# Offset convolution by minimal filtering of row pairs in a deformable-convolution kernel

## Chip, cores and metric

The kernel runs on one core of one Trainium2 chip. The metric is the device time of one execution in microseconds (us); the kernel before takes 1758.54 us (median of 3 runs, 1754.74 to 1759.95). The profiled execution spans 1756.5 us, and all times on the page count from its start. Engines: PE is TensorE (PEld its weight loads), DVE VectorE, ACT ScalarE, POOL GpSimd, SP the engine that issues most DMAs.

## What is computed

Two layers on a batch of 8 images of 128 channels and 64 x 64 pixels, all float32. Only the first is touched. Its steps, cut to what matters:

```python
xn  = group_norm(x)                                  # per image
om  = conv3x3(xn, off_w) + off_b                     # 128 -> 27 channels: THE OFFSET CONVOLUTION
off = om[:, :18].reshape(B, 9, 2, H, W)              # dy, dx of each of 9 taps at each pixel
mask = sigmoid(om[:, 18:])
py, px = row + ky - 1 + off_y, col + kx - 1 + off_x  # where each tap samples
val = bilinear(xn, py, px) * mask                    # 4 corners, zero outside the image
y   = einsum('bckhw,ock->bohw', val, w) + b          # deformable convolution, 128 -> 128
x   = x + relu(batch_norm(y) * gamma + beta)
# second layer: group norm, a 3x3 convolution with routed and mixed expert weights, residual
```

## The kernel before

The first layer is `dense()`. Each image is cut into 11 bands of 6 rows and each band into 11 blocks of 6 columns. For one block DVE multiplies row and column tents into sampling weights (`weights`), PE multiplies them with the block's pixels (`sample`), ACT copies the samples out of PSUM, and PE makes the deformable convolution of the band before (`conv`). The tents come from the offsets, through tables in device memory. The offset convolution and these tables are made by a generator, `tables(b)`, of which a step or two is taken in each block, so that the tables of an image are made while the image before it is sampled; image 0's run alone at the start.

```python
def weights(n):                                    # DVE, one per block
    s = a6.tile([P, TAPS, T, T], F32, name="s")    # a6: 6 buffers
    nc.vector.tensor_tensor(s[0:QQ], x_wts[...], y_wts[...], ALU.mult)

def sample(n):                                     # PE and ACT, one per block
    nc.tensor.matmul(pq, lhsT=xts[g][0:QQ, c], rhs=s, start=True, stop=True)
    nc.scalar.copy(samples[g % 2][...], pq)

def finish(g, py):                                 # one per band
    y = a3.tile([P, T, W], F32, name="y")          # a3: 3 buffers
    nc.scalar.activation(y[:, first:], py[:, first:], AF.Identity, bias=db_sb)
    yield
    nc.vector.bn_stats(ystats[:, b, j, :], flat)
    ...                                            # and the DMA of y to device memory

for g in range(len(bands) + 1):                    # the band loop
    ...
    for c in range(NT1):                           # 11 blocks
        weights(n + AHEAD)                         # AHEAD = 3
        sample(n)
        ...                                        # loads of the tables two bands ahead (POOL)
        next(ended, None)                          # a step of finish(g - 1)
        if g and c > 1:
            conv(g - 1, c - 2, py)
        next(turned, None)                         # pixels of band g + 1: transposes on PE
        for _ in range(1 + (c % 3 == 2)):          # 14 steps of tables in a band
            next(made, None)
```

The part of `tables(b)` that the change replaces, with what stands around it. `pad` holds the image, normalised in place, with rows of zeros above and below. Four matmuls with 32 output partitions each fill the four quarters of one PSUM tile, one for each quarter of the image:

```python
# ... load of the image, its statistics, scale and shift
for c in range(0, NCH, 2):                         # NCH = 8, 512 pixels each
    nc.scalar.activation(part[c], part[c], AF.Identity, bias=shift, scale=scale)
    nc.vector.tensor_scalar(part[c + 1], part[c + 1], scale, shift, ALU.mult, ALU.add)
    yield
if b == 0:
    for t in (y_wts[1], x_wts[1], x_wts[2]):
        nc.vector.memset(t, 0.0)
yield from pause(2)
def evacuate(c, pc):
    nc.scalar.activation(omr[:, c * CH : (c + 1) * CH], pc, AF.Identity, bias=offb_sb)
    nc.vector.tensor_scalar(omc[:, :, 8 * c : 8 * c + 8], pc.rearrange(...), offb_sb, None, ALU.add)
done = []
for c in range(2):
    pc = ps_c.tile([P, CH], F32, name="pc")
    for n, k in enumerate((4, 3, 5, 1, 0, 2, 7, 6, 8)):
        ...
        if n == 2 and done:
            evacuate(*done.pop())
        for j in range(4):
            r = 16 * j + 8 * c + ky + ROWPAD - 1
            nc.tensor.matmul(pc[32 * j : 32 * j + 32]..., lhsT=offw_sb[:, k, :],
                             rhs=pad[:, r : r + 8, lo + kx - 1 : hi + kx - 1],
                             start=(n == 0), stop=(n == TAPS - 1))
        if n % 2:
            yield from pause(5)
    yield from pause(3)
    done.append((c, pc))
evacuate(*done.pop())
yield from pause(4)
# ... DMAs of omr and omc to device memory, the reduction `most`, pause(9),
# ... loads into off_y, mask, off_x, pause(14), sigmoid of the mask,
for i in range(NR):                                # 5 tents: two ops of ACT, three of DVE,
    ...                                            # two stores each, two double buffers, 4 steps
```

Of the kernel before, what the change touches and what calls it, by code (L numbers as in the profile page):

```python
# [8 lines left out]
F32 = mybir.dt.float32  # L9
I32 = mybir.dt.int32  # L10
AF = mybir.ActivationFunctionType
ALU = mybir.AluOpType
# [4 lines left out]
P = 128  # L17
H = W = 64
HW = H * W
HP = WP = H + 2  # L20
TAPS = 9
NT = HW // P
CH = 512
# [22 lines left out]
WB = W + 2  # L46
ROWPAD = REACH + 1
NQI = H + 2 * ROWPAD
YSTEP = TAPS * WB
# [4 lines left out]
WP6 = W + 2 * ROWPAD  # L54
# [3 lines left out]
def deform_moe_conv(  # L58
# [18 lines left out]
    nc = tc.nc  # L77
# [91 lines left out]
    def dense():  # L169

        with ExitStack() as st:
            st.enter_context(tc.manual_schedule())
            a1 = st.enter_context(tc.tile_pool(name="d1", bufs=1))
            a2 = st.enter_context(tc.tile_pool(name="d2", bufs=2))
            a3 = st.enter_context(tc.tile_pool(name="d3", bufs=3))
            a6 = st.enter_context(tc.tile_pool(name="d6", bufs=6))
            ps_c = st.enter_context(tc.tile_pool(name="ps_c", bufs=2, space=PSUM))
            ps_q = st.enter_context(tc.tile_pool(name="ps_q", bufs=3, space=PSUM))
            ps_y = st.enter_context(tc.tile_pool(name="ps_y", bufs=1, space=PSUM))
# [9 lines left out]
                nc.gpsimd.memset(t[:, NT1 - 1, :, Q - ROWPAD :], 0.0)  # L189
            offw_sb = a1.tile([P, TAPS, 32], F32, name="offw_sb")  # L190
            nc.gpsimd.memset(offw_sb[:, :, 27:32], 0.0)
            offb_sb = a1.tile([P, 1], F32, name="offb_sb")
            nc.gpsimd.memset(offb_sb, 0.0)
            ident = a1.tile([P, P], F32, name="ident")
# [6 lines left out]

            off_y = a1.tile([WB, 3, 3, WB], F32, name="off_y")
            mask = a1.tile([WB, 3, 3, WB], F32, name="mask")
            off_x = a1.tile([WB, TAPS * (WP6 - 1) + ROWPAD], F32, name="off_x")
            for t in (off_y, mask, off_x):
                nc.gpsimd.memset(t, 0.0)


            x_wts = [a1.tile([P, NT1, T, TAPS, T], F32, name=f"xwts{i}") for i in range(3)]
            y_wts = [a1.tile([P, T, TAPS, WB], F32, name=f"ywts{i}") for i in range(2)]
# [10 lines left out]
            def tables(b):  # L223
# [4 lines left out]
                def pause(n):  # L228
                    for _ in range(n):
                        yield  # L230
# [3 lines left out]
                pad = pads[b % 2]  # L234
                others = (nc.sync, nc.sync) if b else (nc.scalar, nc.gpsimd)
                for q in range(4):
                    rows = slice(16 * q, 16 * q + 16)
# [39 lines left out]
                for c in range(0, NCH, 2):  # L277
# [2 lines left out]
                        part[c + 1], part[c + 1], scale, shift, ALU.mult, ALU.add  # L280
                    )
                    yield
                if b == 0:
                    for t in (y_wts[1], x_wts[1], x_wts[2]):
                        nc.vector.memset(t, 0.0)
                yield from pause(2)

                om = a1.tile([P, 2, HW // 4], F32, name="om", tag="om")
                omr = om[:, 0]
                omc = om[:, 1].rearrange("p (w h) -> p w h", w=W)  # L290

                def evacuate(c, pc):
                    nc.scalar.activation(
                        omr[:, c * CH : (c + 1) * CH], pc, AF.Identity, bias=offb_sb
                    )
                    nc.vector.tensor_scalar(
                        omc[:, :, 8 * c : 8 * c + 8],
                        pc.rearrange("p (h w) -> p w h", w=W),
                        offb_sb, None, ALU.add,
                    )  # L300

                done = []
                for c in range(2):
                    pc = ps_c.tile([P, CH], F32, name="pc")

                    for n, k in enumerate((4, 3, 5, 1, 0, 2, 7, 6, 8)):
                        ky, kx = divmod(k, 3)
                        lo, hi = max(0, 1 - kx), min(W, W + 1 - kx)
                        if n == 2 and done:
                            evacuate(*done.pop())  # L310
                        for j in range(4):
                            r = 16 * j + 8 * c + ky + ROWPAD - 1
                            nc.tensor.matmul(  # L313
                                pc[32 * j : 32 * j + 32].rearrange("p (h w) -> p h w", w=W)[
                                    :, :, lo:hi
                                ],
                                lhsT=offw_sb[:, k, :],
                                rhs=pad[:, r : r + 8, lo + kx - 1 : hi + kx - 1],
                                start=(n == 0),
                                stop=(n == TAPS - 1),  # L320
                                skip_group_check=True,
                            )
                        if n % 2:
                            yield from pause(5)
                    yield from pause(3)
                    done.append((c, pc))
                evacuate(*done.pop())
                yield from pause(4)
                for j in range(4):
                    nc.sync.dma_start(  # L330
# [7 lines left out]
                nc.vector.tensor_reduce(  # L338
                    most[:, b : b + 1], omr, AX.X, ALU.max, apply_absolute_value=True
                )  # L340
                yield from pause(9)
                for k in range(3):
                    rows = slice(k, k + H)
# [23 lines left out]
                else:  # L367
                    tents = []
                    for t in samples:
                        flat = t.rearrange("p k r w -> p (k r w)")  # L370
# [169 lines left out]

            LOADS = 17
            made, later = tables(0), tables(1)
            for _ in range(LOADS):
                next(made)
# [5 lines left out]
            def reach():  # L550
# [6 lines left out]
                nc.vector.tensor_reduce(count, pn[0:1], AX.X, ALU.add)  # L557
                nc.vector.tensor_copy(count_i, count)

            nc.sync.dma_start(out=dw_sb, in_=dw)  # L560
            for t, src in ((db_sb, db), (gamma_sb, gamma), (beta_sb, beta)):
                nc.sync.dma_start(out=t, in_=src)
# [20 lines left out]
            for g in range(len(bands) + 1):  # L583
                b, j = bands[g] if g < len(bands) else (B, 0)
                if g:
                    py = ps_y.tile([P, T, W], F32, name="py")
                if j == NT1 - 2:
                    for _ in made:
                        pass
                    made = tables(b + 2) if b + 2 < B else iter(())  # L590
                turned = pixels(g + 1) if g + 1 < len(bands) else iter(())
                for c in range(NT1):
                    if g < len(bands):
                        n = g * NT1 + c
# [260 lines left out]
    def layer1():  # L855
# [6 lines left out]
        with ExitStack() as st:  # L862
# [266 lines left out]
            for f, *args in todo:  # L1129
                f(*args)  # L1130

    dense()
    layer1()
    near_all = nc.values_load(count_i[0:1, 0:1], min_val=0, max_val=18 * 4 * B)
# [53 lines left out]
```

## Time and profile before

All times are of the profiled execution.

| stretch (us from the start) | what runs | PE busy | DVE busy |
|---|---|---|---|
| 0 to 76 | image 0: load, normalisation, offset convolution, tables | 23.16 | 29.75 |
| 76 to 1370 | the 88 bands, with the tables of images 1 to 7 in the first 76 of them | 1277.35 | 855.23 |
| 1370 to 1427 | start of the second layer | 20.57 | 48.37 |
| 1427 to 1757 | second layer | 322.50 | 256.34 |

How to read it. The page gives busy time for each engine, then the span in 40 slices, where a digit is the busy share in tenths; then the chain of work that ended last, as shares of the span. A row of the groups names line, engine, operation, output and inputs with partitions x elements, and the count; behind the bar are busy time and the mean of one in ns; behind the second bar the time for which the engine was idle just before, and what ended it. A float32 matmul stands in the trace as two instructions, so its counts are doubled. In a timeline each row is a start, a duration, the engine and the instruction, with equal neighbours merged.

### The profile page before, as it was taken

What the parts mean: (1) busy time and instruction counts of PE and PEld (TensorE: products, weight loads), DVE (VectorE), ACT (ScalarE), POOL (GpSimd) and SP (SyncE); (2) the same over time, 40 slices, a digit from 0 to 9 for tenths busy, and PEclk for the clock granted to TensorE, in tenths of its full rate; (3) what the DMA queues carried; (4) which work ended last, traced back from release to release, by engine and by line L of the source; (5) the groups of instructions that cost most, each with busy time, mean ns of one, the idle gap of its engine ahead of it and who ended that gap; (6) DMA issues with size and microseconds to landing.
All of it is one profiled execution on the core that took longest, in us unless ns stands there. A gap on an engine that the chain in (4) does not pass through costs nothing. (4 is left out here: it accounts for less than half of the span.)

```text
span 1756.5 us, 21264 instructions
## 1 busy us (share of the span) xinstructions
PE 1643.6 (94%) x6490; PEld 931.0 (53%) x6490; DVE 1189.7 (68%) x1910; ACT 944.4 (54%) x1970; POOL 939.6 (53%) x1516
## 2 busy tenths in 40 slices
PE   4399999999999999999999999999999479999998
PEld 2155565566566556655665666566666234444443
DVE  4464874687467648755874587477665688888882
ACT  1465765576476557655765676476665323333330
POOL 3375576558557746764675657557763322322210
PEclk9599999999999999999999999999999689999999
DMA  4643774585368438744863675376663603444311
GB/s 133 124 121 93 154 179 106 115 194 137 93 133 203 121 82 168 180 106 103 193 150 94 134 187 143 98 137 151 161 158 87 267 25 144 155 156 154 123 49 62
DMA packets 197598, 235.84 MB, mean 134 GB/s; under 512 B 133964, under 2 KB 148048, under 8 KB 197478
## 3 DMA queue, kind: packets, MB, share of 16 engines
q0 software_dynamic: 94976, 124.94, 32.4%
q1 hardware_dynamic: 100556, 109.04, 20.7%
q8 instruction: 57, 0.93, 0.2%
q10 hardware_dynamic: 1946, 0.41, 0.1%
q14 instruction: 63, 0.52, 0.1%
HBM read 183.00 MB, written 50.82 MB: 133 GB/s over the span
## 5 line engine op out<-in xcount | busy, mean ns | idle before, releaser
L495 DVE TENSOR_TENSOR s<-xwts,ywts 100x324 f32<-100x324 f32 x968 | 691.5, 759 | 186.4 <-PE pq L506 160.1
L506 PE MATMUL pq<-s,xt 100*128 100x324 f32 x1936 | 696.8, 441 | 12.4 <-DVE s L495 6.7
L512 ACT COPY samples<-pq 128x324 f32<-128x324 f32 x968 | 423.9, 443 | 463.8 <-PE pq L506 458.1
L521 PE MATMUL py<-samples,dw_sb 128*128 128x384 f32 (+1 forms) x1584 | 625.1, 476 | 2.2 <-ACT y L532 2.1
L441 POOL DMA_DIRECT2D xwts<-tabx x863 | 527.2, 621 | 96.9 <-DMA ywts<-taby 52.6
L425 POOL DMA_DIRECT2D ywts<-taby x528 | 302.4, 587 | 365.8 <-DVE s L495 309.4
L506 PEld LDWEIGHTS pq<-s,xt 100*128 100x128 f32 x1936 | 322.4, 190 | 185.9 <-issue 48.7
L521 PEld LDWEIGHTS py<-samples,dw_sb 128*128 128x128 f32 x1584 | 299.5, 189 | 138.5 <-ACT y L532 6.5
L478 PE MATMUL pt<-ident,picked 128*100 128x128 f32 x968 | 194.2, 275 | 41.8 <-ACT picked L465 33.7
L478 PEld LDWEIGHTS pt<-ident,picked 128*100 128x100 f32 x968 | 121.6, 128 | 181.7 <-issue 80.0
L535 DVE BATCH_NORM_STATS2 ystats<-y 128x6 f32<-128x384 f32 (+1 forms) x88 | 48.2, 547 | 218.5 <-ACT y L532 218.5
L1102 PE MATMUL pc<-v,u 128*128 128x512 f32 x384 | 172.8, 599 | 9.2 <-DVE u L1051 9.2
L1102 PE MATMUL pc<-v,wmix 128*128 128x512 f32 x384 | 176.4, 605 | 0.0
L485 ACT COPY xt<-pt 100x512 f32<-100x512 f32 (+1 forms) x264 | 147.5, 559 | 2.2 <-PE pt L478 2.2
L313 PE MATMUL pc<-pad,offw_sb 128*32 128x504 f32 (+1 forms) x1152 | 142.2, 601 | 1.9 <-ACT pad L278 1.9
L1102 PEld LDWEIGHTS pc<-v,u 128*128 128x128 f32 x384 | 72.4, 190 | 98.3 <-issue 85.1
L1080 ACT ACTIVATE t<-pc,bmix 128x512 f32<-128x512 f32 x32 | 22.0, 687 | 182.5 <-issue 94.3
L1102 PEld LDWEIGHTS pc<-v,wmix 128*128 128x128 f32 x384 | 72.3, 191 | 88.6 <-issue 84.9
L457 ACT COPY picked<-pad 128x900 f32<-128x900 f32 x88 | 91.7, 1042 | 9.0 <-DMA xwts<-tabx 9.0
L608 ACT COPY samples<-samples 128x1188 f32<-128x1188 f32 x80 | 95.9, 1198 | 0.0
L930 POOL TENSOR_TENSOR x<-x,xt 128x512 f32<-128x512 f32 x32 | 47.0, 1496 | 85.3 <-ACT x L928 85.3
L930 POOL TENSOR_TENSOR pad<-pad,pad 128x512 f32<-128x512 f32 x28 | 39.6, 1442 | 71.6 <-ACT pad L928 71.5
(137 smaller groups left out, 897.1 us busy)
## 6 DMA issues: line engine op xcount, KB each, us to landing
ywts<-taby POOLq DMA_DIRECT2D x528, 116.0 KB, 4.3
pad<-in_x_dram SPq DMA_DIRECT2D x48, 512.0 KB
xwts<-tabx POOLq DMA_DIRECT2D x173, 116.0 KB, 3.8
out_dram<-yo SPq DMA_DIRECT2D x32, 512.0 KB
xwts<-tabx POOLq DMA_DIRECT2D x172, 92.8 KB, 3.8
yd<-y SPq DMA_DIRECT2D x80, 192.0 KB
xwts<-tabx POOLq DMA_DIRECT2D x173, 69.6 KB, 3.6
pad<-yd SPq DMA_DIRECT2D x16, 512.0 KB
```

Source lines behind the costliest of these rows:

```text
L313: nc.tensor.matmul(pc[32 * j : 32 * j + 32].rearrange("p (h w) -> p h w", w=W)[:, :, lo:hi], lhsT=offw_sb[:, k, :], rhs=pad[:, r : r + 8, ...
L425: engine.dma_start(out=y_wts[g % 2][r * Q : (r + NR) * Q, r].rearrange("p b c -> p (b c)"), in_=bass.AP(tensor=y_table[b].tensor, offset=y ...
L441: engine.dma_start(out=x_wts[g % 3][q:QQ:Q, :, lo:hi].rearrange("p t a b c -> p t (a b c)"), in_=bass.AP(tensor=x_table[b].tensor, offset= ...
L457: nc.scalar.copy(picked[g % 2][:, 1 : NT1 - 1], bass.AP(tensor=one.tensor, offset=one.offset, ap=[list(one.ap[0]), [T, NT1 - 2], [W, Q], [ ...
L478: nc.tensor.transpose(pt[0:QQ, c], picked[g % 2][:, c0 + c].rearrange("p y x -> p (y x)"), ident,)
L485: nc.scalar.copy(xts[g][0:QQ, c0 : c0 + n], pt[0:QQ, 0:n])
L495: nc.vector.tensor_tensor(s[0:QQ], x_wts[g % 3][0:QQ, c].rearrange("p a k r -> p k r a"), y_wts[g % 2][0:QQ, :, :, T * c : T * c + T].rear ...
L506: nc.tensor.matmul(pq.rearrange("p k r a -> p (k r a)"), lhsT=xts[g][0:QQ, c], rhs=ss.pop(n)[0:QQ].rearrange("p k r a -> p (k r a)"), star ...
L512: nc.scalar.copy(samples[g % 2][:, :, 2 : T + 2, T * c : T * c + T], pq)
L521: nc.tensor.matmul(py[:, first:], lhsT=dw_sb[:, 3 * ky + kx], rhs=samples[g % 2][:, n, first + ky : T + ky, kx : kx + W], start=(i == 0), ...
L608: nc.scalar.copy(samples[g % 2][:, :, 0:2], samples[(g - 1) % 2][:, :, T : T + 2])
L1102: nc.tensor.matmul(pc, lhsT=us[j][:, kx], rhs=vs[g][:, rows, kx : kx + W], start=(kx == 0), stop=(kx == 2),)
```

## The change

For two output rows that lie below each other, a filter of three rows needs four input rows d0 to d3. Written out, that is six products with filter rows g0, g1, g2. Minimal filtering does it with four:

```
m0 = (d0 - d2) * g0            m1 = (d1 + d2) * (g0 + g1 + g2) / 2
m2 = (d2 - d1) * (g0 - g1 + g2) / 2            m3 = (d1 - d3) * g2
even row = m0 + m1 + m2        odd row = m1 - m2 - m3
```

Each product is a convolution along the row with three taps. In place of 2 chunks x 9 taps = 18 groups of four matmuls for an image there are 4 products x 3 taps = 12, of the same shape. It is for relieving PE. The row combinations (d0 - d2 and so on) are made by DVE, in two halves of 1024 elements for each product, and the four products are put together by ACT (one) and DVE (four operations); the copy `omc`, transposed within the tile, is made by ACT in one piece. The combined weights are made once, by POOL.

Two combination buffers of 8 KB in each partition need room: `off_y`, `mask` and `off_x` become views of one of them, and the buffers of `s` go from 6 to 5, those of `y` from 3 to 2. The zeroing of the three vanishes; the zeroing of other weight tiles moves behind the offset convolution of image 0. The second layer is untouched.

```diff
-            a3 = st.enter_context(tc.tile_pool(name="d3", bufs=3))
-            a6 = st.enter_context(tc.tile_pool(name="d6", bufs=6))
+            a3 = st.enter_context(tc.tile_pool(name="d3", bufs=2))
+            a6 = st.enter_context(tc.tile_pool(name="d6", bufs=5))
@@
+            offu_sb = [a1.tile([P, 3, 32], F32, name=f"offu_sb{i}") for i in range(2)]
@@
-            off_y = a1.tile([WB, 3, 3, WB], F32, name="off_y")
-            mask = a1.tile([WB, 3, 3, WB], F32, name="mask")
-            off_x = a1.tile([WB, TAPS * (WP6 - 1) + ROWPAD], F32, name="off_x")
-            for t in (off_y, mask, off_x):
-                nc.gpsimd.memset(t, 0.0)
+            combos = [a1.tile([P, H // 2, W], F32, name=f"combo{i}") for i in range(2)]
+            flat = combos[1].rearrange("p h w -> p (h w)")
+            off_y, mask = (flat[0:WB, i * YSTEP : (i + 1) * YSTEP]... for i in range(2))
+            off_x = flat[0:WB, 2 * YSTEP : ...]
@@ in tables(b): evacuate() and the loop over chunks and taps go; instead
+                two = omr.rearrange("p (t i w) -> p t i w", i=2, w=W)
+                even, odd = two[:, :, 0], two[:, :, 1]
+                def combine(j):                      # DVE, two halves, one step each
+                    lo, hi, op = ((0, 2, ALU.subtract), (1, 2, ALU.add),
+                                  (2, 1, ALU.subtract), (1, 3, ALU.subtract))[j]
+                    for half in range(2):
+                        rows = [pad[:, ROWPAD - 1 + H // 2 * half + i :][:, 0 : H // 2 : 2]
+                                for i in (lo, hi)]
+                        nc.vector.tensor_tensor(combo_of[j][:, half * n : half * n + n], *rows, op)
+                        yield
+                combo_of = {1: combos[0], 2: combos[1], 0: combos[0], 3: combos[1]}
+                weight_of = {0: offw_sb[:, 0:3], 1: offu_sb[0], 2: offu_sb[1], 3: offw_sb[:, 6:9]}
+                def tap(j, kx):                      # PE, four matmuls
+                    ...
+                        nc.tensor.matmul(pcs[j][32 * q : 32 * q + 32]..., lhsT=weight_of[j][:, kx],
+                            rhs=combo_of[j][:, 8 * q : 8 * q + 8, lo + kx - 1 : hi + kx - 1],
+                            start=(kx == 1), stop=(kx == 2))
+                for j in (1, 2):
+                    yield from combine(j)
+                yield from pause(2)
+                tap(1, 1); tap(1, 0)                 # (written on one line here)
+                yield from pause(6)
+                tap(1, 2); tap(2, 1)
+                yield from pause(3)
+                nc.scalar.activation(even, taken(1), AF.Identity, bias=offb_sb)
+                yield from combine(0)
+                yield
+                tap(2, 0); tap(2, 2)
+                yield from pause(3)
+                m2 = taken(2)
+                nc.vector.tensor_tensor(odd, even, m2, ALU.subtract)
+                nc.vector.tensor_tensor(even, even, m2, ALU.add)
+                yield
+                yield from combine(3)
+                tap(0, 1); tap(0, 0)
+                yield from pause(6)
+                tap(0, 2); tap(3, 1)
+                yield from pause(3)
+                nc.vector.tensor_tensor(even, even, taken(0), ALU.add)
+                yield from pause(3)
+                tap(3, 0); tap(3, 2)
+                yield from pause(4)
+                nc.vector.tensor_tensor(odd, odd, taken(3), ALU.subtract)
+                yield
+                nc.scalar.copy(omc, omr.rearrange("p (h w) -> p w h", w=W))
                 yield from pause(4)
@@ the zeroing of y_wts[1], x_wts[1], x_wts[2] (image 0) moves behind the reduction `most`
@@ once, at the start
+            u1, u2 = offu_sb
+            nc.gpsimd.tensor_tensor(u2, offw_sb[:, 0:3], offw_sb[:, 6:9], ALU.add)
+            nc.gpsimd.tensor_tensor(u1, u2, offw_sb[:, 3:6], ALU.add)
+            nc.gpsimd.tensor_tensor(u2, u2, offw_sb[:, 3:6], ALU.subtract)
+            for u in offu_sb:
+                nc.gpsimd.tensor_scalar(u, u, 0.5, None, ALU.mult)
```

## Prediction, made before the changed kernel ran

> **What bounds the kernel now.** I read the page from the slices down. Rows of section 2:
>
> ```profile
> PE   4399999999999999999999999999999479999998
> DVE  4464874687467648755874587477665688888882
> PEclk9599999999999999999999999999999689999999
> ```
>
> PE stands at 9 from the third slice to the 31st and again in the second layer; the clock granted is full there. DVE is at 4 to 8 with a rise in each image. So in the band loop PE sets the time, and the question is whether a PE time taken out is really gained, or DVE fills it. The chain that ended last, in order of time, agrees where no tables are made:
>
> ```profile
> 1293.94 0.65 PE py L521 x2
> 1306.99 0.65 PE py L521 x2
> 1320.04 0.65 PE py L521 x2
> ```
>
> One such row in each band, 13.05 us apart: a band without table work is 13.05 us of PE (11 samples of 0.55, 9 deformable taps of 0.65 and 11 transposes that come to 1.2 together; the spacing of starts in the timeline). In a stretch with table work the chain lists the offset convolution itself:
>
> ```profile
> 1103.47 1.84 PE pc L313 x16
> 1105.31 0.74 PE pq L506 x2
> 1109.43 0.98 PE pc L313 x8
> 1110.41 0.74 PE pq L506 x2
> ```
>
> x16 is two taps (4 quarters, 2 passes each for float32), x8 is one. What a pair of taps costs the stream I take from starts in PE's timeline, since the durations of matmuls overlap:
>
> ```profile
> 931.99 0.81 PE L521 MATMUL py<-samples,dw_sb 128*128 128x384 f32 x2
> 932.73 1.90 PE L313 MATMUL pc<-pad,offw_sb 128*32 128x504 f32 x16
> 934.55 0.81 PE L506 MATMUL pq<-s,xt 100*128 100x324 f32 x2
> 935.20 0.81 PE L521 MATMUL py<-samples,dw_sb 128*128 128x384 f32 x2
> ```
>
> From py to the next pq is 2.56 us here and 0.65 elsewhere, so 1.91 more; from pq to py it is 0.65 here and 0.55 elsewhere, 0.10 more. A pair costs 2.01 us. The single tap (starts 945.08, 945.82, 946.80) costs 1.72 - 0.65 + 0.10 = 1.17 us. An image has 8 pairs and 2 singles: 8 x 2.01 + 2 x 1.17 = **18.4 us**. As a check, two images start their offset convolutions at 919.33 and 1082.94, 163.6 us apart; 11 bands of 13.05, less 2 for the first band's shorter rows, plus 18.4 are 160.0. The other 3.6 us are small statistics matmuls and waits in the stretch of the tents.
>
> **What the Trainium skill says.** "TensorEngine Tiling (Array Packing)", Key Properties, says that a change of the tiling mode drains the array. The trace agrees: 0.09 and 0.10 us before and after each group of quarter-width taps. Fewer groups save that too. "VectorE: DVE Perf Modes", in the section on the errata, gives (N+151)/0.96 ns for a float32 tensor_tensor: 1257 ns at 1056 elements. The trace has 1246 (median of line 1022), so 1024 elements should take some 1.21 us. "SBUF — State Buffer", Who interferes with whom, says that a DVE operation with two SBUF inputs contends with a GpSimd instruction that reads SBUF. In the bands POOL almost only issues DMAs, and its issues take 0.61 us (median) beside a DVE that is doing just such operations, so I count nothing for it.
>
> **The change on PE.** All 12 groups come in pairs: 6 x 2.01 = 12.1 us an image in place of 18.4, **6.36 us less**. Images 1 to 7 lie in the band loop: 7 x 6.36 = **44.5 us**, if PE is fed.
>
> **On DVE.** Added for each image: 8 combinations x 1.21 = 9.7 us and 4 joins from PSUM of some 0.68 (line 1088, the same shape, has 680 ns), 2.7. Removed: 2 evacuations of 0.75. Net 10.9 us an image. Does it fit? Rows of the windows view (length, then busy times of PE, PEld, DVE, ACT, POOL) over the offset convolution and over the tents:
>
> ```profile
> 920.00:986.00 66.00, 66.00 (x329) 34.07 (x322) 30.85 (x45) 33.43 (x74) 34.42 (x59) 1.00 0.39 96
> 1182.00:1195.00 13.00, 11.80 (x46) 7.21 (x46) 13.00 (x22) 9.82 (x22) 9.32 (x16) 1.00 0.86 198
> ```
>
> During the offset convolution DVE is busy for 31 of 66 us; 11 more are 42 of some 60. In the tents it is full and PE loses 1.2 us in 13, but no combination falls there. More important is how DVE waits, in order, for others:
>
> ```profile
> DVE ystats L535 <- ACT y L532: 218.5, 79, 6.6
> DVE s L495 <- PE pq L506: 160.1, 215, 2.7
> DVE om L296 <- ACT om L293: 51.0, 15, 6.9
> ```
>
> DVE runs ahead of PE until it stands still at each band's statistics, 2.8 us each time, or lacks a free buffer of s. I place the new steps by counting steps of the generator, 14 to a band: the four first combinations fall in blocks 9, 10, 0 and 1, just ahead of the statistics of block 1, so their 4.8 us mostly replace a wait. The first of combine(0), in block 10, waits for tap(1,2) of block 8, some 2.7 us, with five products s ready, 6 us of samples. The joins with m2 come three steps behind their taps. Nowhere do I find the three products ahead used up; in the worst place (the two combinations of one block behind two joins, 3.8 us) PE is in a stretch with 2 us of taps. The 51 us of waits at the old evacuations vanish; four shorter ones an image come.
>
> **On ACT.** Two evacuations of 0.70 become one, plus a copy of 1024 elements: line 608 copies 1188 in 1.20, so some 1.05 us, perhaps more for its strided reads. About +0.4 us an image; three PSUM buffers of samples hide it.
>
> **Buffers.** With 5 of s, DVE's lead is one block (1.2 us) smaller. That costs only in the tents, where DVE falls behind: at most 1.2 us an image. y's second buffer is needed again after 13 us, while its DMA takes a few. The generator has 142 steps in place of 147 (the convolution itself 45 in place of 50), so tables are ready sooner. Stated cost of lead, waits and jitter: 0 to 1.3 us an image, I take 0.65, **4.5 us** in all.
>
> **Image 0**, alone at the start. Before, ACT and DVE have normalised at 16.0, PE starts at 13.94 and the stores go out at 33.67 and 34.46. After: PE can't begin until the first combination is there, about 17; combinations, products and joins then alternate (tap 1 to 21.5, with the clock still low; tap 2 to 24, joins to 25.5, combine(3) to 28, its taps to 30, join and copy to 32). The stores go out some 2 us sooner, though PE's taps fall by a third. Against that stands POOL: three zeroings of 1.8 us fall, five small operations come (a one-element one takes 0.71), which must wait for the offset weights' load, and POOL's power for the scale stands behind them in order. I count **0.5 us** gained. The 9 us of zeroing on DVE then lie beside the round trip through device memory, in which DVE is idle for 10.7 us, so just beside it.
>
> Sum: 1758.5 - 44.5 - 0.5 + 4.5 = **1718 us**, 2.3% less.
>
> **Rivals.** (1) *DVE becomes the bound*: the burst of combinations empties the products ahead and PE waits for s. For it speaks that DVE is already full in the tents and at 7 and 8 in the slices; against it the 31 of 66 us and the standing wait at the statistics. If every combination cost PE half its time, 7 x 5 = 35 us would come back: 1749. (2) *A wait between engines*: taps now wait for DVE, DVE for taps (a combination buffer is used twice), joins for PSUM. A block's wait of 2 us at three places an image is 42 us: 1756. Against it: each step stands 3 to 6 generator steps (2 to 4 blocks) from what it needs. (3) *Shared storage*: off_y, mask and off_x now lie in the second combination buffer. If their nine loads waited for one another as parts of one tile, ACT would stand at the sigmoid and with it all sample copies, over 10 us an image: 1790. Against it: the three stores into the old off_x, whose extents don't overlap, were issued without waiting, two back to back at 41.25, while those into off_y, which do overlap, came 3.8 us apart; so waits follow extents, and the three views don't overlap. (4) *The freed time goes elsewhere*: POOL's loads or the DMA engines set the bands. Bands without taps run at 13.05 us with the same loads, so hardly.
>
> **Range and chances.** Full gain without loss would be 1712, and a better start 1708. Half of rival 1 or 2 gives about 1735. The line for 2% is 1723.4, only 5 us above my number. So: 1718, range 1707 to 1737; faster by over 2% 0.64, within 2% 0.33, slower by over 2% 0.03.
>
> **What would show it.** Right: the busy time of the offset taps falls by about a third (142 to about 95 us); starts of two images' convolutions lie 157 to 158 us apart; bands without tables stay at 13.05; PE's waits for s and samples (12.4 us before pq) hardly grow; the combinations take 1.2 us. Wrong in rival 1: idle time of PE at pq, put down to DVE's s, of tens of us. In rival 2: PE or DVE idle at the taps, combinations and joins, with PE's slices falling to 8 in each image. In rival 3: ACT waits for the loads of mask. The weakest terms are the loss of 4.5 us, which I read off an order of steps and not off a trace, and the start.

## The result, and the profile after

The changed kernel takes 1703.9 us (median of 4 runs, 1701.86 to 1710.82) against 1756.64 before: ratio 0.9707, 95% interval 0.9671 to 0.9743. That is 2.9% less, faster by more than 2%. The prediction said 1718 and 1707 to 1737: the direction is right, the size is not, and the time lies below the range.

The slices of the changed kernel (section 2 of its page; one digit is a tenth of busy time):

```profile
PE   3299999999999999999999999999999479999998
DVE  6586777678687868776786878686664888888882
PEclk9599999999999999999999999999999689999999
```

PE still stands at 9 through the band loop, at full clock. DVE has risen where it had been at 4 and 5. So PE remained the bound, with less work. The groups show the change's own operations (out <- in, shape, count | busy us, mean ns | idle time just before):

```profile
L312 DVE TENSOR_TENSOR combo<-pad 128x1024 f32<-128x1024 f32 x64 | 77.4, 1227 | 8.5 <-PE pc L329 8.5
L375 ACT COPY om<-om 128x1024 f32<-128x1024 f32 x8 | 16.0, 2002 | 9.2 <-DVE om L373 9.2
```

A combination takes 1.23 us (1.21 was predicted) and before all 64 of them DVE waited for PE's taps only 8.5 us in total. The transposing copy on ACT takes 2.00 us, twice my 1.05.

PE's timeline around one pair of taps (start, duration) has the old spacing: 2.57 us from py to the next pq, of which 0.65 are usual, then 0.65 to py in place of 0.55. A pair costs 2.02 us, as before:

```profile
902.15 0.81 PE L572 MATMUL py<-samples,dw_sb 128*128 128x384 f32 x2
902.89 1.90 PE L329 MATMUL pc<-combo,offu_sb 128*32 128x504 f32 x16
904.72 0.81 PE L557 MATMUL pq<-s,xt 100*128 100x324 f32 x2
905.37 0.81 PE L572 MATMUL py<-samples,dw_sb 128*128 128x384 f32 x2
```

The windows view over one offset convolution (length, then busy times of PE, PEld, DVE, ACT, POOL) shows what DVE took over: 49 us of 65, against 31 of 66 before.

```profile
875.00:940.00 65.00, 64.56 (x307) 36.63 (x306) 48.94 (x69) 39.73 (x84) 38.36 (x65) 1.00 0.46 107
```

And the waits that answer to the three shown of before:

```profile
DVE s L546 <- PE pq L557: 172.3, 286, 2.7
DVE ystats L586 <- ACT y L583: 100.4, 73, 6.5
DVE combo L312 <- PE pc L329: 8.5, 7, 2.1
```

DVE's wait for the statistics fell from 218.5 to 100.4 us, but not by the combinations alone. A later run (e3) has only the change's smaller numbers of buffers, and its two waits are:

```profile
DVE s L495 <- PE pq L506: 244.1, 332, 2.7
DVE ystats L535 <- ACT y L532: 130.6, 77, 6.5
```

With fewer buffers of s, DVE stands more at PE's samples and less at the statistics. Against that run the two waits together fall from 374.7 to 272.7 us: the combinations took DVE's standing time, more of it at the samples (72 us) than at the statistics (30 us). The 51 us at the old evacuations are gone.

### Where the 52.7 us lie

ACT copies y once in each band, right behind the band's last deformable tap. Successive starts of this copy measure the bands; an image's number is that of the image being sampled. Summed over the two profiles (1756.5 and 1703.8 us):

| part | before | after | difference |
|---|---|---|---|
| up to the first copy of y | 101.94 | 101.73 | -0.2 |
| four bands with the offset convolution (mean, images 1 to 6) | 69.89 | 63.33 | -6.56 each |
| two bands with the tents (the same) | 28.05 | 26.96 | -1.09 each |
| other bands (13.05 each, one of 13.50) | | | 0.0 |
| from the last copy of y to the end | 385.8 | 386.8 | +1.0 |

The first and last row differ by less than equal code does from profile to profile (some 2 us at the start, up to 6 at the end). The bands in which image 1's tables are made (under image 0's samples) save 7.56 us, those of each later image 7.65 (6.56 + 1.09). In all the bands save 53.5 us: about 46 in the convolution, 7.6 in the tents. The convolution is what I predicted. The tents should have cost something, and they gained. Their bands, in ACT's timeline, before (first fence) and after, from one copy of y to the next, with the fifth column tent's row among them (idle time before, in brackets):

```profile
1005.57 0.58 ACT L532 ACTIVATE y<-py,db_sb 128x384 f32<-128x384 f32 x1
1019.57 0.58 ACT L532 ACTIVATE y<-py,db_sb 128x384 f32<-128x384 f32 x1
1024.85 0.81 ACT L402 ACTIVATE work<-off_x,steps 66x594 f32<-66x594 f32 x1 [1.91 <-DMA tabx<-work]
1033.52 0.59 ACT L532 ACTIVATE y<-py,db_sb 128x384 f32<-128x384 f32 x1
```

```profile
961.46 0.58 ACT L583 ACTIVATE y<-py,db_sb 128x384 f32<-128x384 f32 x1
972.86 0.82 ACT L453 ACTIVATE work<-combo,steps 66x594 f32<-66x594 f32 x1 [0.57 <-DMA tabx<-work]
975.18 0.58 ACT L583 ACTIVATE y<-py,db_sb 128x384 f32<-128x384 f32 x1
988.05 0.58 ACT L583 ACTIVATE y<-py,db_sb 128x384 f32<-128x384 f32 x1
```

Twice 13.05 are 26.10; before it was 14.00 + 13.95, after 13.72 + 12.87. On the mean of the six images the first band takes 14.04 before and 14.10 after, the second 14.01 and 12.86: the gain lies in the second. There the fifth tent stood before; after, the tents begin earlier, one of them in the band ahead, which still takes 13.05, and none of ACT's work on them is left for the second. A row of the waits view names a candidate for the cost: a column tent of ACT can't be written before the store of the tent two earlier has landed. Before (with the wait of PE that goes with it), then after:

```profile
ACT work L402 <- DMA tabx<-work: 16.4, 13, 2.6
PE pq L506 <- ACT samples L512: 5.7, 6, 1.6
```

```profile
ACT work L453 <- DMA tabx<-work: 7.4, 10, 1.3
```

ACT works in order, so behind such a wait the copies of samples stand too, and then PE. The six waits of PE lie in the second tent band, one in each image: where ACT waited 1.2 us for the store, PE was idle 0.2 us; where ACT waited 2.6, PE was idle 1.6 and the band took 14.61. They come to 0.95 us an image, of the 1.15 gained there. The changed kernel has no such row of PE; in its first tent band PE waits for the copies of the transposes instead, by 0.2 to 0.9 us in five of the images.

### The profile page after: what moved, and what is told of

Its sections match the earlier page's. It is cut to its first block, busy times and chain, and to the rows that moved or that the text cites. A ratio compares the mean times of both kernels' runs of the same rounds, so it can differ in the third digit from the quotient of the medians.

```text
span 1703.8 us, 20572 instructions
## 1 busy us (share of the span) xinstructions
PE 1591.8 (93%) x6106; PEld 918.3 (54%) x6106; DVE 1280.1 (75%) x1990; ACT 954.9 (56%) x1970; POOL 938.3 (55%) x1518
## 5 line engine op out<-in xcount | busy, mean ns | idle before, releaser
L546 DVE TENSOR_TENSOR s<-xwts,ywts 100x324 f32<-100x324 f32 x968 | 706.6, 761 | 205.3 <-PE pq L557 172.3
L586 DVE BATCH_NORM_STATS2 ystats<-y 128x6 f32<-128x384 f32 (+1 forms) x88 | 48.3, 549 | 100.4 <-ACT y L583 100.4
L312 DVE TENSOR_TENSOR combo<-pad 128x1024 f32<-128x1024 f32 x64 | 77.4, 1227 | 8.5 <-PE pc L329 8.5
```

What stands on the lines that cost most here:

```text
L546: nc.vector.tensor_tensor(s[0:QQ], x_wts[g % 3][0:QQ, c].rearrange("p a k r -> p k r a"), y_wts[g % 2][0:QQ, :, :, T * c : T * c + T].rear ...
```

## The experiments

Twelve runs. "Tents" is the mean of the two tent bands, "convolution" that of the four, both over images 1 to 6 of the profile, in us; ratios are to the kernel before as run beside each set (medians 1754.54 to 1758.99), with 95% intervals.

| run | median us | ratio | convolution | tents |
|---|---|---|---|---|
| before | 1756.64 | 1 | 69.89 | 28.05 (27.64 to 28.57) |
| after | 1703.9 | 0.9707 (0.9671 to 0.9743) | 63.33 | 26.96 (26.59 to 27.46) |
| e1: after, tents 5 steps later | 1707.23 | 0.9732 (0.9715 to 0.9748) | 63.33 | 27.37 (26.94 to 27.85) |
| e2: before, tents 5 steps earlier | 1750.02 | 0.9970 (0.9958 to 0.9983) | 69.89 | 26.75 (26.57 to 26.98) |
| e3: before, fewer buffers | 1757.42 | 1.0007 (0.9996 to 1.0018) | 69.89 | 27.77 (26.88 to 28.80) |
| e7: e3 and a third column-tent buffer | 1748.82 | 0.9959 (0.9943 to 0.9976) | 69.90 | 27.18 (26.44 to 28.11) |
| e5: after, combinations twice | 1733.08 | 0.9872 (0.9855 to 0.9888) | 66.58 | 26.66 (26.42 to 26.99) |
| e6: after, tents spread | 1700.61 | 0.9689 (0.9673 to 0.9705) | 63.33 | 26.10 (26.10 to 26.11) |
| e8: after, third tent buffers | 1698.79 | 0.9674 (0.9652 to 0.9696) | 63.33 | 26.28 (26.23 to 26.50) |
| e9: after, taps in threes | 1704.12 | 0.9732 (0.9679 to 0.9786) | 62.66 | 26.69 (26.51 to 26.94) |
| e11: before, tents earlier and spread | 1742.45 | 0.9915 (0.9889 to 0.9942) | 69.89 | 26.10 (26.09 to 26.11) |
| e10: after, spread, third buffers, threes | 1704.2 | 0.9695 (0.9665 to 0.9725) | 62.90 | 26.10 (26.09 to 26.11) |
| e13: after, spread and third buffers | 1698.74 | 0.9675 (0.9655 to 0.9695) | 63.32 | 26.16 (26.09 to 26.51) |
| e12: e10 and 4 steps more for the loads | 1694.04 | 0.9654 (0.9637 to 0.9671) | 62.91 | 26.23 (26.22 to 26.23) |

### First round: the place of the tents, or the buffers?

The change has 142 generator steps in place of 147, so its tents begin at block 8 of a band and not at block 1. **e1** puts the five steps back:

```diff
-                yield from pause(14)
+                yield from pause(19)
                 nc.scalar.activation(mask, mask, AF.Sigmoid)
```

> The changed kernel with five more generator steps ahead of the tents, so that they begin at block 1 of a band as before the change, and not at block 8. In each of images 1 to 7 the two bands with the tents took 28.05 us before and 26.96 after (mean, from the starts of the copies of y), 26.10 without tables. Theory 'place of the tents' (the gain beyond the taps comes from where the steps fall): back to about 28, total 1711 us. Rival 'buffers or loads' (the gain comes from something else in the change): it stays at 27.0 and at 1704 us.

The tents rose to 27.37, not to 28. So the place gives back 0.41 of the 1.09 us in the changed kernel; both expectations missed. ACT's waits for the column stores rose with it, from 7.4 to 12.0 us. By band it is clearer: the second rose from 12.86 to 13.88, nearly the 14.01 of before, and PE's waits for sample copies are back in it, 4.9 of 5.7 us:

```profile
PE pq L557 <- ACT samples L563: 4.9, 6, 1.2
```

The first band fell at the same time, from 14.10 to 13.49, below the 14.04 of before; this no run explains.

**e2** takes five steps out of the old convolution:

```diff
                         if n % 2:
-                            yield from pause(5)
-                    yield from pause(3)
+                            yield from pause(5 - c)
+                    yield from pause(3 - c)
```

> The kernel before with five generator steps taken out of the second chunk of its offset convolution, so that its tents begin at block 8; the same 18 groups of taps and the same buffers. Theory 'place of the tents': the two tent bands fall from 28.05 to about 27.0 us, the total by 7.6 to about 1749. Rival 'buffers or loads': no change, 1757.

Here the place alone brings 28.05 down to 26.75, in every image, below the changed kernel's 26.96. Over six images that is 7.8 us; the second band takes 12.86, as in the changed kernel, and PE's row of waits for sample copies is gone. But the bands of image 0 took 2.7 us more, and the total fell by 0.3%. The waits for the column stores fell from 16.4 to 4.6 us. No minimal filtering is in this kernel.

**e3** changes the buffers alone (`bufs` 3 to 2 and 6 to 5, as in the change's diff):

> The kernel before with 5 buffers of s and 2 of y, nothing else. The prediction's term for DVE's shorter lead: up to 1.2 us an image more in the tent bands, 4.5 us in all, 1761. Theory 'place of the tents': no effect, 28.05 us in the tent bands and 1757. Rival 'buffers': the tent bands fall to 27 and the total to 1749.

No effect on the time (ratio 1.0007), and 27.77 lies within the scatter of its images. The cost that I had put on DVE's shorter lead isn't there, and the buffers don't bring the gain either.

**e7** uses the freed room for a third buffer of the column tents:

```diff
-                    work = a1.tile([WB, 2, 2, YSTEP], F32, name="work", tag="om")
-                    tents = [[work[:, a, i % 2] for i in range(NR)] for a in range(2)]
+                    work = a1.tile([WB, 5, YSTEP], F32, name="work", tag="om")
+                    tents = [[work[:, i % 2] for i in range(NR)], [work[:, 2 + i % 3] for i in range(NR)]]
```

> The kernel before with 5 buffers of s and 2 of y, and the room used for a third buffer of the column tents, so that ACT's tent need not wait for the store of the tent two earlier (16.4 us of such waits in all before). If those waits of ACT are what costs PE its time in the tents: tent bands from 28.05 down to about 27, total 1750 or less. If instead DVE, full in the tents, is what costs it: no change, 28 and 1757.

ACT's waits for column stores vanish from the list. The tents fall to 27.18, 0.59 less than in e3, and the total by 0.4%. The images scatter (26.44 to 28.11), so the totals of e3 and e7 are the better evidence: their intervals don't overlap. So those waits are part of the loss, not all of it.

### Second round: room on DVE, density, groups of taps

**e5** writes each combination twice (the same `tensor_tensor` once more):

> The changed kernel with every combination computed twice: 9.8 us more of DVE in each image, in the same places of the convolution's four bands (63.33 us, images 1 to 6). If DVE has room there, as the prediction holds: 63.3 still and 1704. If DVE was about to become the bound (rival 1): up to 9.8 us an image, 73 us for the four bands and 1770.

In between, and it shows where the room ends. Of the 9.8 us added to an image, 3.25 came out in the four bands, all of it in the second, where the first four combinations stand (17.46 to 20.7 us); the other four stayed hidden. PE now waits there, as its timeline shows (idle time before, in brackets):

```profile
913.92 0.78 PE L560 MATMUL pq<-s,xt 100*128 100x324 f32 x2 [1.20 <-DVE s L549]
920.37 0.78 PE L560 MATMUL pq<-s,xt 100*128 100x324 f32 x2 [1.57 <-DVE s L549]
```

So the burst of the first four has room for 4.9 - 3.25 = some 1.6 us more. Together with the tents, images 1 to 6 lost 2.96 us each, 17.8 in all. The rest of the profile's 33 us (1736.9 against 1703.8) came early: 7.8 us up to the first copy of y, where nothing hides DVE, and 7.5 in the bands that make image 1's tables, which I did not follow further.

**e6** gives each tent one step more:

```diff
                         store(i - 1)
-                    yield from pause(2)
+                    yield from pause(3)
```

> The changed kernel with one generator step more behind each of the five tents: the same work over 5 more blocks' steps. If it is the density of the tents (DVE busy all the time, stores close behind each other) that makes their bands longer: the loss of 0.86 us an image over 26.10 falls below 0.3, total 1700. If the loss comes from the mere number of operations of ACT and DVE in their order: unchanged, 26.96 and 1704.

The loss vanishes: 26.10 in each image, what two bands take without any tables. The same DVE and ACT operations are there, only less close together, so it is their density that cost PE time. No wait for column stores is left either; whether these or DVE's full queue are the cost, this run doesn't separate (e8 does). The total gained less (3 us) because image 1's tables, which have a shorter run-up, lack the steps: its bands took 2.4 us more.

**e8** gives both tents three buffers in the changed kernel, without spreading them:

```diff
-                    work = a1.tile([WB, 2, 2, YSTEP], F32, name="work", tag="om")
-                    tents = [[work[:, a, i % 2] for i in range(NR)] for a in range(2)]
+                    work = a1.tile([WB, 3, YSTEP], F32, name="work", tag="om")
+                    colw = combos[0].rearrange("p h w -> p (h w)")
+                    tents = [[work[:, i % 3] for i in range(NR)],
+                             [colw[0:WB, (i % 3) * YSTEP : (i % 3 + 1) * YSTEP] for i in range(NR)]]
```

> The changed kernel with three buffers instead of two for the row and for the column tents (the column tents lie in the first combination buffer, which is free by then). If ACT's waits for the stores of the tents (7.4 us in all) are what costs PE its time there: the loss of 0.86 us an image falls to 0.4 or less, total 1700. If DVE's full queue is the cause: unchanged, 1704.

26.28: four fifths of the loss in the changed kernel go with the buffers alone, while DVE has as much to do in the two bands (22.8 us, against 23.0). In that kernel the waits for the stores were the larger part.

**e9** groups the taps by product, three at a time:

```diff
-                tap(1, 1); tap(1, 0)
-                yield from pause(6)
-                tap(1, 2); tap(2, 1)
+                taps(1)                    # kx = 1, 0, 2
+                yield from pause(7)
...                                         # likewise taps(2), taps(0), taps(3); 41 steps as before
```

> The changed kernel with its 12 taps in 4 groups of three, each product in one go, instead of 6 pairs; the same number of generator steps. Each group costs 0.19 us of changes of the tiling mode by the prediction's reading, so two groups less save 0.4 us an image: 62.9 us for the four bands, total 1701. Rival: 2.8 us of PE without a sample starve ACT and then stop PE at the samples' PSUM buffers: 64 us or more, 1710.

The convolution falls by 0.67 us an image to 62.66, more than the 0.4 expected (0.33 for each group saved, where the prediction's reading gave 0.19), and PE waits for no sample copy, so ACT isn't starved. But the runs scatter (1698 to 1719), and in the profile one band took 15.9 us in place of 13.05. There the sigmoid held ACT up for 3.08 us, waiting for a load of the offsets:

```profile
488.75 0.70 ACT L406 ACTIVATE combo<-combo 66x594 f32<-66x594 f32 x1 [3.08 <-DMA combo<-rowwise]
```

### Third round: the sum, and the old kernel with its tents put right

**e11** spreads the tents of the kernel before and moves them (the edits of e2 and e6):

> The kernel before with one step more behind each tent, and five steps less in the second chunk of its offset convolution (147 steps as before). If the loss in the tents is only a matter of where steps fall, and not of the change: tent bands from 28.05 to 26.1, total 1757 - 7 x 1.95 = 1743; the change would then be worth about 44 us against it, the taps alone. If the old layout keeps a loss of its own: above 27 us, 1749 or more.

26.10 in every image, 1742.45 us. So the loss in the tents was never a property of the convolution. Against this version the changed kernel with spread tents (e6) is 1742.45 - 1700.61 = 41.8 us faster, and 45.1 us in the bands of the two profiles: about what minimal filtering brings by itself.

**e10** puts e6, e8 and e9 together (pauses between the groups 6, 6, 5 and 4 in place of 7, 7, 7 and 5):

> The three edits together on the changed kernel: three buffers for both tents, one step more behind each tent, taps in four groups of three (five pauses' steps taken out between the groups, so that the generator keeps its 142 steps). By the sum of the single runs: 26.1 us in the two tent bands, 62.66 in the four bands of the convolution, that is 0.86 + 0.67 us less an image than the changed kernel, 7 x 1.53 = 10.7 us: 1693. If the triples leave ACT behind and the tents then meet late loads (one band of 15.9 us in the run with triples alone): 1698 or more.

The second case came: runs from 1696 to 1712. Tents and convolution are at 26.10 and 62.90, but single bands took up to 1.5 us more, before the sigmoid. ACT's timeline shows one such place:

```profile
792.12 0.70 ACT L406 ACTIVATE combo<-combo 66x594 f32<-66x594 f32 x1 [2.29 <-DMA combo<-rowwise]
```

**e13** leaves the taps in pairs:

> The changed kernel, its taps in pairs, with three buffers for both tents and one step more behind each: tent bands at 26.10, the convolution at 63.33, image 0 some 2 us longer as in the run with the spread alone. Total 1698 to 1700, close to each of the two edits alone, since each takes nearly all of the 0.86 us an image that is there to take.

As expected, 1698.74: each of the two edits takes nearly all there is, and they don't add. One band of its profile took 14.56 us, where the sigmoid waited 1.34 us for a load, so late loads don't come with the triples alone.

**e12** adds four steps for the loads to e10:

```diff
-                yield from pause(14)
+                yield from pause(18)
                 nc.scalar.activation(mask, mask, AF.Sigmoid)
```

> The kernel with the three edits (triples, three buffers, spread tents) and four steps more between the loads of the offsets and the sigmoid. In the run before, ACT waited up to 2.29 us for the mask's load in some images, and single bands took 0.6 to 1.5 us more; its runs lay between 1696 and 1712. If late loads cause the scatter: single bands at 13.05, all runs within some 4 us, median 1694 to 1697 (image 0's tables are a few steps short and cost about 2 us). If the scatter comes from elsewhere: again up to 1712.

The bands are even again, the runs lie between 1690 and 1695: late loads were what scattered e10. In its profile the sigmoid waits for loads only in image 0, at the start. With 1694.04 us, ratio 0.9654, this is the lowest ratio of all, worth some 9 us against the changed kernel's; its interval overlaps those of e8 and e13.

## Why the prediction was wrong, point by point

- **PE as the bound, and the taps: right.** 6 x 2.01 in place of 8 x 2.01 + 2 x 1.17 gave 6.36 us an image; 6.56 were measured. The rest is the first pair before, which met a late copy of ACT and cost some 2.3. In all 46 us for my 44.5.
- **DVE's room: right, though not quite where I saw it.** I counted on DVE's waits at the statistics; of their fall, 88 us come with the smaller numbers of buffers alone (e3), which moved the standing time to the samples, and there the combinations took most of it. e5 gives the margin that I could not: about 1.6 us at the first four, all of a doubled load at the others.
- **Image 0: not resolved.** 0.2 gained for 0.5, but five profiles with the changed kernel's start have their first copy of y between 101.1 and 103.2. The row stores went out 0.9 us sooner, the column stores 0.3 later, since ACT's copy took 2.0 us.
- **Rivals: none came.** (1) and (2): in the bands PE waited 0.3 us for products of DVE, and some 7 us for the transposes' copies and y (8 before). The 5.7 us that it had waited for sample copies are gone. (3): the issues of the row offsets' loads waited for one another 41.5 us in all, before it was 39.3 + 3.6 (off_y and mask), so the shared buffer added none. (4): bands without tables stayed at 13.05.
- **The failing step is "Buffers"**: "Stated cost of lead, waits and jitter: 0 to 1.3 us an image, I take 0.65, 4.5 us in all." Sign and size are wrong: the tents gained 1.09 us an image. e3 shows that the shorter lead costs nothing. I had the cause in hand, "The generator has 142 steps in place of 147", and took from it only that tables are ready sooner. I did not follow it to the tents, whose loss of 2 us an image in the kernel before I had seen (3.6 us unexplained in the check of 163.6 against 160.0) and taken as given. By e1, e2, e6 and e11 that loss depends on where the tents stand and how close they lie. What the runs show in place of the cost: with five steps fewer the fifth tent, at which ACT waits for a store and PE for ACT, leaves the second tent band, which then takes 12.86 us and not 14.01.
- **The sum.** I counted 40.5 us saved and the profiles differ by 52.7. The 12.2 between are 4.5 of cost that isn't there, 7.6 gained in the tents and 1.4 more at the taps, less 0.3 at the start and 1.0 at the end. A further 2 us of the distance from 1718 to 1704 is no effect of the change: the kernel before took 1758.54 when I wrote, 1756.64 beside the result.
- **The range was cut at its lower end for the same reason**: "Full gain without loss would be 1712" holds only if no existing loss can shrink (and by my own terms it is 1758.5 - 44.5 - 0.5 = 1713.5). Without the tents' gain the time would have been near 1711.

What stays open: the first tent band. In the second, the place explains the gain: 1.02 us come back with it in the changed kernel (e1), and in the old one it takes away all of it (e2). The first takes 14.04 before, 14.10 after, 13.89 in e2, but 13.49 in e1, whose tents begin at the same step as before the change; fewer buffers alone (e3) give 13.93 (13.39 to 14.49 over the images), and nothing else was separated.

## What to carry to other kernels

Where a kernel's side work is dealt out by counting steps, a change of the number of steps moves everything behind it: follow each later stage to its new place, since it can be worth more than a term that one has worked out carefully. A stretch that is longer than its bound is a loss that a change can also take away; give it a range on both sides. And before crediting a change with all that it measures, put its side effect into the old kernel: here some 42 to 46 of 53 us were the filtering, and moving and spreading the tents gave the old kernel about 15 us without it.

## What the runs showed that I had not expected

A copy of ACT that reads with a stride of 64 floats took 2.00 us for 1024 elements, while one of 1188 elements in rows takes 1.20. Spreading 5 tents by one step each brought two bands from 26.96 to exactly 26.10, although DVE and ACT had slightly more work in them (DVE 23.4 us in place of 23.0). And an in-order engine that waits 2.3 us for one load costs a band up to 1.5 us, even with three PSUM buffers of samples between it and PE.
